# A ConvNeXt block with a gate: 8-channel convolution matrices read in one piece, four buffers, and another order of loads

## The chip, the cores and the metric

The kernel runs on one core of a Trainium2 chip. The metric is device time in microseconds (us). The program has five engines that matter: TensorE (PE, matmuls and the weight loads that go with them, PEld), VectorE (DVE), ScalarE (ACT), GpSimd (POOL) and SyncE (SP, which here only issues DMAs). Each works through its own instructions in order, and they meet by semaphores. DMAs run on 16 DMA engines that the core's queues share.

## The reference

Input x is 32 images of 384 channels and 28 x 28 pixels, float32. The first layer is a ConvNeXt block:

```python
y = conv_general_dilated(x, dw_w, padding=[(3, 3), (3, 3)], feature_group_count=C)  # 7x7, each channel alone
y = y.transpose(0, 2, 3, 1) + dw_b
y = layernorm(y) * ln_g + ln_b
y = gelu(y @ w1 + b1)                      # 384 -> 1536
gx = sqrt(sum(y * y over pixels)); nx = gx / (mean(gx) + eps)
y = grn_g * (y * nx) + grn_b + y
y = y @ w2 + b2                            # 1536 -> 384
x = x + y.transpose(0, 3, 1, 2)
```

The second layer takes mean, maximum and minimum of each channel's plane, forms logits from them with small matrices (W1, W2_1, W2_2, W3, Wfc) and returns sigmoid(logits + x).

## The kernel before

The kernel has two stages. The first computes the depthwise convolution of all images and writes it to a scratch tensor in HBM. The second goes through the images one by one: normalisation, the product with w1, GELU, the response norm, the product with w2, the gate. Both big products use a scheme with fewer multiplications, which needs sums of blocks of w1 and w2 (15 sums each, `UPSTEPS` and `STEPS`). These sums ("forms") are made in the first stage by POOL (`form_w`) and stored to the scratch tensors `u1d` and `u2d`. The change touches the first stage only.

**The convolution as matmuls.** For one channel a plane is cut into strips of 4 rows (`RW`), 7 strips an image; rows are padded to 32 columns, so a strip is 128 numbers, on the 128 partitions. For one channel the seven strips of all 32 images form the moving operand, 128 x 224. The output strip is a matrix times the strip itself (L309), plus a matrix times the next strip (L310, only 96 output rows wide), plus a matrix times the strip before (L313). All three are windows of one banded 128-row table whose row p is one and the same row of numbers, shifted by p. That row is written once for each channel to the scratch tensor `fs` (448 floats a channel, mostly zeros, built in `tab` from the 7x7 weights), and `load_t` (L199) reads it with a step of one element from partition to partition. One `load_t` brings the matrices of 8 channels (`TC`) into one of three `tmat` buffers: for each partition 8 pieces of 320 floats, behind 32 columns that are set to zero once.

**Steps and blocks.** The main loop has 48 steps of 8 channels; four steps are a block of 32 channels (`XC`). In each step PE does 24 convolution products, and ACT (L327) and DVE (L319) evict them from PSUM, with the bias `dwb` added, into `yc`, which is stored to `yd` every second step (the last two such stores go to `yl`).

**Turning x.** x comes from HBM as groups `xi` of 32 channels x 4 images (392 KB, `load_x`, four buffers); 8 groups are a block. POOL copies a group into a padded buffer `xpad` (`pad_x`, L237, two buffers), PE transposes it in two parts of 4 and 3 strips (`turn_x`, L248), and DVE copies each from PSUM into `xt` (L253). Before the main loop the first 8 groups are turned; in the loop two groups of the next block are turned in each step, between the convolution's products.

**Order.** The program is written as one sequence, and a scheduler puts each engine's instructions in an order by data and priority. DMAs of this stage are issued by SP, in order. SP starts with dww (the 7x7 weights), cv (five vectors of 384, in pieces of 4 bytes), dwb, the first xi, three stores to fs, one xi, two tmat loads, two xi, w1s (all of w1, 2304 KB), eight xi, w2s (all of w2) and fv (three vectors of 1536). In the loop the load of the matrices of step s + 2 is issued at step s. Step s makes one form, of w1 in even steps and of w2 in odd ones, from step 4 to 33. awt, w22b and wfc, small tensors for the gate, are loaded behind the stage in the program's text.

Of the kernel before, what the change touches and what calls it, by code (L numbers as in the profile page):

```python
# [8 lines left out]
F32 = mybir.dt.float32  # L9
AF = mybir.ActivationFunctionType  # L10
# [3 lines left out]
P = 128  # L14
C = 384
CB = C // P
FF = 4 * C
FB = FF // P
# [4 lines left out]
R = 8  # L23
# [8 lines left out]
PW = P // RW  # L32
XC = 32
TC = 8
YC = 16
NB = P // XC
REACH = 3 * PW
MW = P + 2 * REACH
FL = MW + P
NLAST = XC // YC  # L40
# [41 lines left out]
NS = len(STEPS)  # L82
# [19 lines left out]
KT = FB // 3  # L102
# [11 lines left out]
def convnext_gate_kernel(  # L114
# [13 lines left out]
    nc = tc.nc  # L128
    B = x.shape[0]
    N = NJ * B  # L130

    const = ctx.enter_context(tc.tile_pool(name="const", bufs=1))
# [7 lines left out]

    fs = [dram.tile([P, FL], F32, name=f"fs_{cb}") for cb in range(CB)]
    NY = C // YC
# [10 lines left out]
    cv = const.tile([P, 5, CB], F32, name="cv")  # L153
    nc.sync.dma_start(cv, cvec.rearrange("v (cb p) -> p v cb", p=P))
    _, lng_t, lnb_t, b2_t, w21_t = (cv[:, i, :] for i in range(5))
    fv = const.tile([P, 3, FB], F32, name="fv")
    b1_t, gg_t, gb_t = (fv[:, i, :] for i in range(3))
    ones_f = const.tile([P, P], F32, name="ones_f")
    nc.gpsimd.memset(ones_f, 1.0 / FF)
    eps_t = const.tile([P, 1], F32, name="eps_t")  # L160
    nc.gpsimd.memset(eps_t, EPS)
# [5 lines left out]
    with ExitStack() as one:  # L167
        tp = one.enter_context(tc.tile_pool(name="tp", bufs=1))
        xip = one.enter_context(tc.tile_pool(name="xip", bufs=4))
        xtp = one.enter_context(tc.tile_pool(name="xtp", bufs=2))  # L170
# [4 lines left out]

        w1s = tp.tile([P, CB, FF], F32, name="w1s")
        w2s = tp.tile([P, FB, C], F32, name="w2s")
        tab = tp.tile([P, CB, FL], F32, name="tab")
        nc.vector.memset(tab, 0.0)

        t0 = REACH + P - 1 - 3 * PW - 3
        for cb in range(CB):
            nc.vector.tensor_copy(
                tab[:, cb, t0 : t0 + 7 * PW].rearrange("p (y x) -> p y x", x=PW)[:, :, :7],
                dww[:, cb, :].rearrange("p (y x) -> p y x", x=7),
            )
            nc.sync.dma_start(fs[cb], tab[:, cb, :])

        NT2 = 3
        T0 = P - REACH
        tmat = [tp.tile([P, TC, T0 + MW], F32, name=f"tmat_{i}") for i in range(NT2)]
        for t in tmat:
            nc.gpsimd.memset(t[:, :, :T0], 0.0)
        dwb = tp.tile([P, C], F32, name="dwb")
        nc.sync.dma_start(dwb, cvec[0:1, :].broadcast_to([P, C]))
        NK = C // TC

        def load_t(s):  # L200
            base = fs[s * TC // P]
            c0 = s * TC % P
            nc.sync.dma_start(
                tmat[s % NT2][:, :, T0:],
                bass.AP(
                    tensor=base.tensor,
                    offset=base.offset + c0 * FL,
                    ap=[[1, P], [FL, TC], [1, MW]],
                ),
            )  # L210
# [29 lines left out]

        def turn_x(i, h, xt):

            g = i % NG
            xv = xt.rearrange("p c (j b) -> p j c b", j=NJ)
            j0, j1 = 4 * h, min(NJ, 4 * h + 4)
            pt = psx.tile([P, 4, P], F32, tag="pt", name=f"pt_{i}_{h}")
            for j in range(j0, j1):
                nc.tensor.transpose(  # L248
                    pt[:, j - j0, :],
                    xpad[i % NPAD][:, j * RW : (j + 1) * RW, :].rearrange("p r w -> p (r w)"),  # L250
                    ident,
                )
            nc.vector.tensor_copy(  # L253
                xv[:, j0:j1, :, g * NB : (g + 1) * NB],
                pt[:, : j1 - j0, :].rearrange("p j (c q) -> p j c q", q=NB),
            )

        def new_xt(k):
            return xtp.tile([P, XC, N], F32, tag="xt", name=f"xt_{k}")

        w1v = w1s.rearrange("p k (t m c) -> p t k m c", m=3, c=P)
        w2v = w2s.rearrange("p (t k) (m c) -> p t k m c", k=3, m=CB)

# [10 lines left out]

        for s in range(2):
            load_t(s)
        for i in range(4):
            load_x(i)
        nc.sync.dma_start(w1s, w1.rearrange("(cb p) f -> p cb f", p=P))
        xt = new_xt(0)  # L280
        for i in range(NG):
            pad_x(i)
            if i + 4 < GT:
                load_x(i + 4)
            for h in range(2):
                turn_x(i, h, xt)
        nc.sync.dma_start(w2s, w2.rearrange("(fb p) c -> p fb c", p=P))
        nc.sync.dma_start(fv, fvec.rearrange("v (fb p) -> p v fb", p=P))
        SK = XC // TC
        GS = NG // SK  # L290
        for s in range(NK):
            k, si = divmod(s, SK)
            if s + 2 < NK:
                load_t(s + 2)
            if si == 0:
# [8 lines left out]
            for c2 in range(TC // 2):  # L304
                pc = psc.tile([P, 2, 256], F32, tag="pc", name=f"pc_{s}_{c2}")
                for ci in range(2):
                    c = 2 * c2 + ci
                    xc = xt[:, si * TC + c, :]
                    nc.tensor.matmul(pc[:, ci, :N], t[:, c, P : 2 * P], xc, start=True, stop=False)  # L309
                    nc.tensor.matmul(  # L310
                        pc[:REACH, ci, : N - B], t[:, c, 2 * P :], xc[:, B:], start=False, stop=False
                    )
                    nc.tensor.matmul(  # L313
                        pc[:, ci, B:N], t[:, c, :P], xc[:, : N - B], start=False, stop=True
                    )
# [18 lines left out]
                if xn is not None:  # L334
                    g, h = divmod(si * (TC // 2) + c2, 2)
                    i = (k + 1) * NG + g
                    if h == 0:
                        pad_x(i)
                        if i + 4 < GT:
                            load_x(i + 4)  # L340
                    turn_x(i, h, xn)
# [19 lines left out]
            if si == SK - 1:  # L361
                xt = xn
            i = s // 2 - 2
            if 0 <= i < NS:
                if s % 2 == 0:
                    form_w(f"u1_{i}", w1v, UPSTEPS[i][1], u1d[:, :, i, :].rearrange("t p c -> p t c"))
                else:
                    form_w(
                        f"u2_{i}", w2v, STEPS[i][1], u2d[i].rearrange("p (t c) -> p t c", c=P)
                    )  # L370

# [19 lines left out]
    nc.vector.memset(gate, 0.0)  # L391
    awt = const.tile([P, 2, CB, R], F32, name="awt")
    nc.sync.dma_start(awt, aw.rearrange("v (cb p) r -> p v cb r", p=P))
    nc.vector.tensor_scalar(gate[:, 0, :, 0:R], awt[:, 0], 1.0 / NT, None, ALU.mult)
    nc.vector.tensor_copy(gate[:, 2, :, 2 * R : 3 * R], awt[:, 1])
    w22b = const.tile([P, R], F32, name="w22b")
    nc.sync.dma_start(w22b, w22.broadcast_to([P, R]))
    grp = const.tile([P, CB, R], F32, name="grp")
# [14 lines left out]
    nc.vector.tensor_copy(gate[:, 1, :, R : 2 * R], grp_b)  # L413
    wfc = const.tile([3 * R, C], F32, name="wfc")
    nc.sync.dma_start(wfc, wfcT)

# [424 lines left out]
```

## Time and profile before

| | us |
|---|---|
| median of 3 runs (3228.82 to 3229.85) | 3229.32 |
| profiled execution, its own time | 3229.09 |
| its span | 3227.3 |
| first convolution matmul (L309) starts | 36.02 |
| last one starts (the second stage's first transposes at 512.29) | 507.5 |
| DMA, share of 16 engines' time / GB/s, 0 to 36 us | 0.85 / 289 |
| the same, 36 to 75.67 us (first block) | 1.00 / 329 |
| the same, 530 us to the end | 0.43 / 137 |

The profile shows one execution, engine by engine; the time of a run is a little longer than the span, by 1.8 us here. A row of the timeline gives start, duration, engine, line, operation, output<-input and count, and in brackets how long the engine stood idle before it and what released it. A row of waits gives the waiting engine and line, what it waited for, us in total, how many times, and the longest. A DMA is shown on its issuing queue (SPq) while it is issued; its data land later: 7.8 us after the issue for tmat in the median, 8.4 for xi, 11.5 for yd.

### The profile page before, as it was taken

To read this page: it belongs to the slowest core of one execution; us is meant where nothing else is said; L and a number is where in the kernel's file an instruction comes from. 1 tells how busy PE (TensorE), PEld (TensorE's weight loads), DVE (VectorE), ACT (ScalarE), POOL (GpSimd) and SP (SyncE) were. 2 spreads that over 40 slices of the span, in tenths; PEclk is the share of its full clock that TensorE was granted. 3 is DMA by queue.
4 is the path that set the end of the run, shared out by engine and by line. 5 is a ranking of instruction groups with operands and counts; after the bars stand their busy time and mean duration, and the time that the engine had idled before them with its cause. 6 is when DMAs were issued, how large, how long until landed. Compare 5 with 4: busy or idle time off the path is not lost.

```text
span 3227.3 us, 35684 instructions
## 1 busy us (share of the span) xinstructions
PE 3177.9 (98%) x12352; PEld 2011.9 (62%) x12352; DVE 1674.7 (52%) x3447; ACT 1881.7 (58%) x3024; POOL 1604.6 (50%) x813
## 2 busy tenths in 40 slices
PE   7999998999999999999999999999999999999998
PEld 6999996555555555555555555555555555555555
DVE  3444335555555555555555555555555555555553
ACT  1222224866666666666666666666666666666662
POOL 2455311555555555555555555555555555555555
PEclk9999998999999999999999999999999999999999
DMA  9999986434444444444444444444444444444333
GB/s 310 342 333 332 317 283 207 129 112 143 141 142 139 136 132 139 142 132 142 145 134 143 145 134 144 134 143 145 145 131 137 131 135 142 141 142 140 123 103 125
DMA packets 300150, 534.10 MB, mean 165 GB/s; under 512 B 121004, under 2 KB 179908, under 8 KB 296900
## 3 DMA queue, kind: packets, MB, share of 16 engines
q1 hardware_dynamic: 287572, 494.51, 47.1%
q10 hardware_dynamic: 12400, 37.33, 3.4%
q8 instruction: 98, 1.61, 0.2%
q14 instruction: 80, 0.66, 0.1%
HBM read 440.65 MB, written 91.13 MB: 165 GB/s over the span
## 4 chain that ended last, share of the span: by engine, by line
PE 87%; ACT 1%; DVE 1%; issue 0%; ACTq 0%; DVEq 0%
PE ph_A L549 13%; PE ph_B L549 13%; PE pz_A L646 11%; PE pz_B L646 10%; PE pz_C L646 5%; PE pz_E L646 5%; PE ph_C L549 5%; PE pz_F L646 3%; PE pz_G L646 3%; PE pz_D L646 3%; PE ph_D L549 3%; PE ph_H L549 3%; PE ph_F L549 3%; PE py L475 2%; PE pc L309 2%; PE pc L310 1%
## 5 line engine op out<-in xcount | busy, mean ns | idle before, releaser
L621 POOL TENSOR_TENSOR d_v<-d_u,y 128x1568 f32<-128x1568 f32 x32 | 112.3, 3511 | 759.5 <-PE pz_B L646 735.4
L524 ACT ACTIVATE y<-y,fv 128x784 f32<-128x784 f32 x384 | 346.7, 941 | 214.5 <-DVE y L564 213.8
L457 ACT ACTIVATE y<-y,fv,gsc 128x784 f32<-128x784 f32 x378 | 358.6, 1027 | 29.9 <-DVE gsc L591 29.9
L327 ACT ACTIVATE yc<-pc,dwb 128x224 f32<-128x224 f32 x192 | 103.7, 642 | 401.1 <-PE pc L313 301.8
L530 ACT ACTIVATE junk<-y 128x784 f32<-128x784 f32 x384 | 326.6, 851 | 5.0
L621 POOL TENSOR_TENSOR d_p<-y 128x1568 f32<-128x1568 f32 x31 | 109.1, 3518 | 434.6 <-ACT y L457 434.6
L549 PE MATMUL ph_A<-af,u 128*128 128x392 f32 x768 | 314.0, 503 | 5.4 <-DVE af L515 5.3
L549 PE MATMUL ph_B<-af,u 128*128 128x392 f32 x768 | 311.3, 493 | 0.3 <-ACT y L556 0.3
L646 PE MATMUL pz_A<-y,u 128*128 128x392 f32 x768 | 268.8, 492 | 0.0
L621 POOL TENSOR_TENSOR y<-d_v,y 128x1568 f32<-128x1568 f32 x64 | 223.5, 3514 | 2.5
L549 PEld LDWEIGHTS ph_A<-af,u 128*128 128x128 f32 x768 | 136.4, 190 | 135.2 <-ACT y L556 57.4
L549 PE MATMUL ph_A<-acc,u 128*128 128x392 f32 x512 | 216.3, 504 | 0.0
L309 PE MATMUL pc<-xt,tmat 128*128 128x224 f32 x768 | 209.3, 354 | 4.9 <-issue 4.9
L549 PE MATMUL ph_B<-acc,u 128*128 128x392 f32 x512 | 213.6, 499 | 0.1
L549 PEld LDWEIGHTS ph_B<-af,u 128*128 128x128 f32 x768 | 145.3, 190 | 109.2 <-DVE y L560 9.6
L646 PEld LDWEIGHTS pz_A<-y,u 128*128 128x128 f32 x768 | 145.8, 190 | 106.4
L556 ACT ACTIVATE y<-ph_A 128x392 f32<-128x392 f32 x256 | 124.7, 487 | 145.2 <-PE ph_A L549 145.1
L560 DVE TENSOR_TENSOR y<-y,ph_A 128x392 f32<-128x392 f32 x128 | 71.9, 562 | 238.9 <-PE ph_A L549 224.6
L446 ACT ACTIVATE sd<-mv,eps_t 128x7 f32<-128x7 f32 x32 | 9.6, 300 | 314.3 <-DVE mv L441 314.3
L515 POOL TENSOR_TENSOR af<-af,acc 128x392 f32<-128x392 f32 x186 | 186.8, 1018 | 4.9
L313 PE MATMUL pc<-xt,tmat 128*128 128x192 f32 x768 | 187.6, 326 | 0.0
L310 PE MATMUL pc<-xt,tmat 128*96 128x192 f32 x768 | 187.6, 326 | 0.0
(153 smaller groups left out, 6903.5 us busy)
## 6 DMA issues: line engine op xcount, KB each, us to landing
u<-u1d SPq DMA_DIRECT2D x128, 960.0 KB, 4.6
u<-u2d SPq DMA_DIRECT2D x480, 256.0 KB, 2.7
tmat<-fs SPq DMA_DIRECT2D x48, 1280.0 KB, 7.8
yd<-yc SPq DMA_DIRECT2D x22, 1792.0 KB, 11.5
yi<-yd SPq DMA_DIRECT2D x32, 1232.0 KB, 6.9
xi<-in_x SPq DMA_DIRECT2D x96, 392.0 KB, 8.4
x<-in_x SPq DMA_DIRECT2D x32, 1176.0 KB, 5.6
out<-x ACTq DMA_DIRECT2D x31, 1176.0 KB, 5.0
```

Of the source, the lines that this page charges most:

```text
L309: nc.tensor.matmul(pc[:, ci, :N], t[:, c, P : 2 * P], xc, start=True, stop=False)
L310: nc.tensor.matmul(pc[:REACH, ci, : N - B], t[:, c, 2 * P :], xc[:, B:], start=False, stop=False)
L313: nc.tensor.matmul(pc[:, ci, B:N], t[:, c, :P], xc[:, : N - B], start=False, stop=True)
L327: nc.scalar.activation(yc[:, :, :, cy + ci].rearrange("p b j -> p j b"), pc[:, ci, :N].rearrange("p (j b) -> p j b", j=NJ), AF.Identity, b ...
L457: eng.activation(out, in_, AF.Identity, bias=add, scale=mul)
L515: eng.tensor_tensor(d, o[in0], o[in1], op)
L524: nc.scalar.activation(y, y, AF.Gelu, bias=b1_t[:, f : f + 1], scale=1.0)
L530: nc.scalar.activation(junk, ys[b][:, f, :], AF.Square, accum_out=ssqs[b][:, f : f + 1])
L549: nc.tensor.matmul(banks[bk][:, :NH], wt[:, i, :], o[opnd], start=(first == 1), stop=True, skip_group_check=True,)
L556: nc.scalar.activation(d, p, AF.Identity)
L621: nc.gpsimd.tensor_tensor(d, o[in0], o[in1], op)
L646: nc.tensor.matmul(pz[:, :NH], wt[:, t, :], o[opnd][:, t, :], start=(first == 1 and t == 0), stop=(t == KT - 1), skip_group_check=True,)
```

## The change

- **fs** is one scratch tensor of 385 rows of 355 floats. The 32 columns of zeros in front of a matrix are part of the row, and the row ends with the last weight (`SN` = 199, `S0` = 156). The 385th row is zeros, since the last partition reads past the 384th. The table is built with one copy for six rows of weights and one for the seventh, and its four stores are issued by ACT.
- **load_t** reads 8 rows as one run of 2840 floats (11360 bytes) for each partition: 128 pieces, not 1024. The zero columns come with it, so the memsets of tmat go. There are four tmat buffers, and the load of step s + 3 is issued at step s.
- **ws** takes the place of w1s and w2s: w1 is loaded into it at step 2, its 15 forms are made in steps 4 to 18, w2 is loaded into the same place at step 19, its forms are made in steps 22 to 36.
- **Order of the first loads**: dww, six xi, tmat 0, four xi, tmat 1, dwb, four xi, tmat 2, tmat 3. There are six xi buffers. fv, cv, both halves of awt, w22b and wfc are loaded in steps 4 to 9.
- **One-element copies by POOL** into the destination hold back such a load until the instruction that wrote the copied element is done: tmat 1 to 3 by a pad, the weights and vectors by the first eviction of the last `yc`.
- In the first 8 groups the second part's copy from PSUM is done by ACT (`turn_x` with `eng`).

```diff
+T0 = P - REACH
+SN = 6 * PW + 7
+S0 = T0 + REACH + P - 1 - 3 * PW - 3
-FL = MW + P
+FL = S0 + SN
...
-    fs = [dram.tile([P, FL], F32, name=f"fs_{cb}") for cb in range(CB)]
+    fs = dram.tile([C + 1, FL], F32, name="fs")
...
-    nc.sync.dma_start(cv, cvec.rearrange("v (cb p) -> p v cb", p=P))
...
-        xip = one.enter_context(tc.tile_pool(name="xip", bufs=4))
+        xip = one.enter_context(tc.tile_pool(name="xip", bufs=6))
...
-        w1s = tp.tile([P, CB, FF], F32, name="w1s")
-        w2s = tp.tile([P, FB, C], F32, name="w2s")
+        ws = tp.tile([P, CB * FF], F32, name="ws")
...
+        NT2 = 4
+        tmat = [tp.tile([P, TC, FL], F32, name=f"tmat_{i}") for i in range(NT2)]
         nc.vector.memset(tab, 0.0)
+        nc.scalar.dma_start(fs[C : C + 1, :], tab[:1, 0, :])
         for cb in range(CB):
             nc.vector.tensor_copy(
-                tab[:, cb, t0 : t0 + 7 * PW].rearrange("p (y x) -> p y x", x=PW)[:, :, :7],
-                dww[:, cb, :].rearrange("p (y x) -> p y x", x=7),
+                tab[:, cb, S0 : S0 + SN - 7].rearrange("p (y x) -> p y x", x=PW)[:, :, :7],
+                dww[:, cb, :42].rearrange("p (y x) -> p y x", x=7),
             )
-            nc.sync.dma_start(fs[cb], tab[:, cb, :])
-        NT2 = 3
-        tmat = [tp.tile([P, TC, T0 + MW], F32, name=f"tmat_{i}") for i in range(NT2)]
-        for t in tmat:
-            nc.gpsimd.memset(t[:, :, :T0], 0.0)
+            nc.vector.tensor_copy(tab[:, cb, S0 + SN - 7 :], dww[:, cb, 42:])
+            nc.scalar.dma_start(fs[cb * P : (cb + 1) * P, :], tab[:, cb, :])
...
-        def load_t(s):
-            base = fs[s * TC // P]
-            c0 = s * TC % P
-            nc.sync.dma_start(
-                tmat[s % NT2][:, :, T0:],
+        def load_t(s, eng=nc.sync):
+            eng.dma_start(
+                tmat[s % NT2].rearrange("p c m -> p (c m)"),
                 bass.AP(
-                    tensor=base.tensor,
-                    offset=base.offset + c0 * FL,
-                    ap=[[1, P], [FL, TC], [1, MW]],
+                    tensor=fs.tensor,
+                    offset=fs.offset + s * TC * FL,
+                    ap=[[1, P], [1, TC * FL]],
                 ),
             )
...
-        for s in range(2):
-            load_t(s)
-        for i in range(4):
+        AHEAD = 6
+        for i in range(AHEAD):
             load_x(i)
-        nc.sync.dma_start(w1s, w1.rearrange("(cb p) f -> p cb f", p=P))
         xt = new_xt(0)
         for i in range(NG):
             pad_x(i)
-            if i + 4 < GT:
-                load_x(i + 4)
+            if i == NG - AHEAD:
+                load_t(0)
+            if i == NG // 2:
+                nc.gpsimd.tensor_copy(tmat[1][:, 0, :1], xpad[i % NPAD][:, 0, :1])
+                load_t(1)
+                nc.sync.dma_start(dwb, cvec[0:1, :].broadcast_to([P, C]))
+            if i + AHEAD < GT:
+                load_x(i + AHEAD)
             for h in range(2):
-                turn_x(i, h, xt)
-        nc.sync.dma_start(w2s, w2.rearrange("(fb p) c -> p fb c", p=P))
-        nc.sync.dma_start(fv, fvec.rearrange("v (fb p) -> p v fb", p=P))
+                turn_x(i, h, xt, (nc.vector, nc.scalar)[h])
+        later = {
+            2: (
+                ws.rearrange("p (cb f) -> p cb f", f=FF),
+                w1.rearrange("(cb p) f -> p cb f", p=P),
+            ),
...
+            9: (wfc, wfcT),
+        }
...
-            if s + 2 < NK:
-                load_t(s + 2)
+            if s + 3 < NK:
+                if s == 0:
+                    for i in range(2, 4):
+                        nc.gpsimd.tensor_copy(tmat[i][:, 0, :1], xpad[i % NPAD][:, 0, :1])
+                        if i == 2:
+                            load_t(i)
+                load_t(s + 3)
+            if s in later:
+                dst, src = later[s]
+                first = dst[:, :1] if len(dst.shape) == 2 else dst[:, 0, :1]
+                nc.gpsimd.tensor_copy(first, yc[: dst.shape[0], 0, 0, :1])
+                nc.sync.dma_start(dst, src)
...
-                        pc[:REACH, ci, : N - B], t[:, c, 2 * P :], xc[:, B:], start=False, stop=False
+                        pc[:REACH, ci, : N - B], t[:, c, 2 * P : T0 + MW], xc[:, B:], start=False, stop=False
...
-            i = s // 2 - 2
+            i = s - U1
             if 0 <= i < NS:
-                if s % 2 == 0:
-                    form_w(f"u1_{i}", w1v, UPSTEPS[i][1], u1d[:, :, i, :].rearrange("t p c -> p t c"))
-                else:
-                    form_w(f"u2_{i}", w2v, STEPS[i][1], u2d[i].rearrange("p (t c) -> p t c", c=P))
+                form_w(f"u1_{i}", w1v, UPSTEPS[i][1], u1d[:, :, i, :].rearrange("t p c -> p t c"))
+            i = s - U2
+            if 0 <= i < NS:
+                form_w(f"u2_{i}", w2v, STEPS[i][1], u2d[i].rearrange("p (t c) -> p t c", c=P))
```

## The prediction

> **What bounds the kernel now.** I read the page first: its busy row, its rows by slice and its chain of waits.
>
> ```profile
> PE 3177.9 (98%) x12352; PEld 2011.9 (62%) x12352; DVE 1674.7 (52%) x3447; ACT 1881.7 (58%) x3024; POOL 1604.6 (50%) x813
> ...
> PE   7999998999999999999999999999999999999998
> ...
> DMA  9999986434444444444444444444444444444333
> ```
>
> TensorE (PE) is busy in 3177.9 of 3227.3 us, so at most 49.4 us can come out without less matrix work, and the change leaves the convolution's products as they are. A slice is 80.7 us: the idle time lies in slice 1 and around slices 7 and 8. The second row to see is DMA: full in the first six slices, 0.3 to 0.5 later. So the conv stage (up to 508 us, where the last L313 ends) has PE and DMA both near full; the rest has only PE. Next the waits of PE. From 36 to 530 us:
>
> ```profile
> PE ph_A L549 <- DVE af L515: 5.3, 1, 5.3
> PE pc L309 <- issue: 4.9, 11, 1.1
> PE py L475 <- ACT yn L457: 4.6, 2, 4.3
> PE pt L248 <- POOL xpad L237: 1.8, 1, 1.8
> ```
>
> The first and third lie after 508 us, in code that the change leaves alone. No wait on a tmat load appears: matrices are never late. Then the timeline of the first 37 us, PE, POOL and SP rows:
>
> ```profile
> 2.91 0.64 SPq L227 DMA_DIRECT2D xi<-in_x  x1
> 8.52 1.00 SPq L203 DMA_DIRECT2D tmat<-fs  x2
> 13.42 0.59 SPq L279 DMA_DIRECT2D w1s<-in_w  x1
> 8.81 1.76 PE L248 MATMUL pt<-ident,xpad 128*128 128x128 f32 x7 [8.81 <-POOL xpad L237]
> 20.88 0.84 POOL L237 COPY xpad<-xi 128x784 f32<-128x784 f32 x1 [9.45 <-DMA xi<-in_x]
> 27.45 1.49 POOL L270 TENSOR_SCALAR u<-w1s 128x512 f32<-128x512 f32 x1 [4.74 <-DMA w1s<-in_w]
> 29.79 6.32 PE L248 MATMUL pt<-ident,xpad 128*128 128x128 f32 x35 [4.77 <-POOL xpad L237]
> 36.02 0.65 PE L309 MATMUL pc<-xt,tmat 128*128 128x224 f32 x2
> ```
>
> The first convolution matmul starts at 36.02. It needs eight groups of x padded, turned and copied (the ninth is turned ahead of it in PE's order). The third group waited 9.45 us for its DMA behind two tmat loads; then POOL, which works in order, sat 4.74 us at a weight form that had been put ahead of the pads, until w1s had landed. Last, a table of stretches (us; then busy PE, PEld, DVE, ACT, POOL; granted clock, DMA share, GB/s):
>
> ```profile
> 11.00:18.00 7.00, 1.76 (x7) 1.36 (x7) 1.36 (x3) 0.00 (x0) 0.43 (x1) 1.00 1.03 354
> 19.00:29.00 10.00, 3.25 (x14) 2.85 (x14) 2.40 (x4) 0.00 (x0) 3.23 (x4) 1.00 1.02 413
> 75.67:115.34 39.67, 39.29 (x248) 37.94 (x248) 16.07 (x25) 8.66 (x16) 12.05 (x12) 1.00 0.99 351
> 523.00:528.50 5.50, 5.50 (x9) 2.94 (x10) 0.33 (x1) 1.49 (x3) 0.00 (x0) 0.51 1.03 388
> ```
>
> The first is mostly tmat traffic in pieces of 1280 bytes, the second x and w1s in rows of 3136 and 6144 bytes. A block of four steps (32 channels) takes 39.67 us, PE full.
>
> **The start.** Removed from in front of x on SP: cv, dwb, three fs stores, two tmat loads and w1s. Up to 36 us the queue listing counts 10.39 MB. In the new order what must land before the first matmul is nine x groups (9 x 0.401 = 3.61 MB), the fs rows (385 x 1420 bytes = 0.55 MB), tmat 0 (128 x 11360 bytes = 1.45 MB) and dww (0.08 MB): 5.69 MB. At 413 GB/s that is 13.8 us. Bytes begin about 1.7 us after the first issue at 0.79 (dww lands 2.0 us after its own), so at 2.5: 16.3. One hole: tmat 0 stands in SP's queue before x groups 7 to 10 and waits until the fs stores, now issued by ACT, have landed. These go out at about 3.5 to 5 us (after dww, as at L183) and took 4.8 us to land, so tmat 0 is issued near 9.5, when SP's six earlier x loads are nearly done; DMA may stand for 2 us. The ninth group lands at 18.3, the eighth at 17.3. The eighth then takes 0.84 us on POOL, 1.76 on PE (the 8.81 row) and about 0.7 for its copy: start at 20.7. Half of the copies of these groups go to ACT. No row shows that copy on ACT; the near one is its eviction acc<-py 128x448, 1.34 us for two, so 0.67 for 128x384, against 0.69 and 0.54 on DVE. Bounds 0.5 and 1.1 (the strided L327 takes 0.64 for 224): once at the end, so 0.7 is taken. ACT has no other work there but its table load (1.28 us).
>
> [...] The trace agrees in the 523 us row (0.51 granted for 5.5 us, after 5.29 us of idleness) and, in durations, at 8.81: 0.25 us for each transpose against 10 in 1.09 us later. While tmat 0 moves PE idles some 4 us, so the turns of groups 7 to 9 and the first matmuls run slow. Before, 6.3 us of transposes warmed PE up first. [...] by the 523 row 2.8; part of it is in the 1.76 already. I add 0.8: effective start 21.5, gain **36.0 - 21.5 = 14.5 us** (bounds 8 to 18). dwb follows tmat 1 and lands near 24; the first eviction is due at about 23. What queues behind it is ACT's evictions and DVE's turns, and four pc banks cover 8 us, so nothing is charged.
>
> **The convolution stage.** PE's rows are unchanged (L310 still 96 wide), 472 us from first to last. What must hold is DMA. A block loads 4 x 1.31 + 8 x 0.401 (x) + 2 x 1.835 (yd) + 4 x 0.262 (forms) = 13.17 MB now, which gives 332 GB/s, as the table's 329 to 351; afterwards 4 x 1.454 makes it 13.75 MB, 346 GB/s. Whether this fits hangs on the tmat rate. [...] 11% more bytes cost 11% more time, 4.11 us a load at 354 against 3.70. The trace has 354 against 413 for longer rows[...]. [...] I take it; it is also close to the 413 row. DMA's block is now busy about 0.98 x 39.67 = 38.9 us, of which tmat 4 x 3.70 = 14.8; with 4 x 3.56 it is 38.3: it fits, and costs nothing. At the other end, 354, it is 24.1 + 16.4 = 40.5, 0.9 over in each block with forms; forms run in 30 of 48 steps, 7.5 blocks, so 6 us are lost. The fourth buffer (a load issued three steps ahead, not two) covers single late loads, not a lack of rate.
>
> The weights move into the stage: ws twice (2.36 MB, 5.7 us each at 413), fv, cv and small ones, with their one-element POOL copies (0.1 us as the memsets). They come at 0.26 MB a step saved (no forms in steps 0 to 3 and 19 to 21), and three steps of prefetched matrices (29 us) cover them. Uncovered, 5 us once each.
>
> POOL: forms come one a step. Now two can run back to back: 10.5 us without a pad from 335.42 on, which is PE's 1.8 us wait above. In the new order at most one five-term form, 1.49 + 4 x 1.27 = 6.6 us, stands between pads (two pairs of short forms, 4.3 us, aside). A pad buffer is free half a step, 4.9 us, before it is due, and the form can start just after the previous pad, half a step earlier than that. So **1.8 us** go. The tmat memsets (0.81 us) lie in POOL's idle start: nothing.
>
> **Sum.** 14.5 + 1.8 = 16.3, less 0.8 for the loads that crowd steps 2 to 9: 15.5. The profiled run is 3229.09 us by its own clock, span 3227.3; span 3211.8, run 3213.6. The median shown is 0.2 above that run: **3213.8**.
>
> **Rivals.** (a) The forecast, 0.68. (b) The start moves less: fs stores on ACT's queue share with x, tmat 0 is issued late, PE cold; start at 28, gain 8 + 1.8 - 0.8 = 9: 3220. For it: the fs landing of 4.8 us. 0.12. (c) More: no hole, start 18.5, and half of the 4.9 us of "issue" gaps go: 17.5 + 1.8 + 2.4: 3207.6; 0.07. (d) Slower: DMA becomes the bound. All partitions of a load read nearly the same 11 KB of HBM, in long runs at once; if that gives 300 GB/s, a load takes 4.85 us, a block 24.1 + 19.4 = 43.5, 3.8 over, 7.5 times = 28.7; less 15.5: 3242.5. It decides below 330 GB/s for tmat (2.07 us over a block). For it: DMA is at 0.97 to 1.0 already. Against it: the old loads read the same bytes together at 354. 0.08. (e) The order changes but the start doesn't, DMA being full from 3 us on: 3227.5 with the POOL wait gone. Against it: 10.4 MB are moved before 36 us, 5.7 needed. 0.05.
>
> A measurement here can tell about 0.2%, 6.5 us, from no change. Faster: a, b, c: 0.87; same 0.05; slower 0.08. The range is 3204 to 3224: it takes in a, b and c and leaves out d and e.
>
> **What would show it.** First L309-type matmul (now L344) at 20 to 22 us; tmat issue to landing under 7.8 us in mid-stage, DMA share in blocks at most as now; last conv matmul near 492; the 1.8 us wait on xpad gone; nothing changed after it. Wrong if PE waits for tmat, or if POOL waits for x in mid-stage.

## The result, and the profile after

| us | before | after | difference |
|---|---|---|---|
| median of 4 runs each on one chip | 3229.59 (3228.82 to 3230.48) | 3217.57 (3216.49 to 3218.74) | -12.0 |
| profiled execution, its own time | 3229.09 | 3216.78 | -12.3 |
| its span | 3227.3 | 3215.1 | -12.2 |
| first convolution matmul starts | 36.02 | 24.40 | -11.6 |
| last convolution matmul row starts | 507.53 | 495.69 | -11.8 |
| from there to the end of the span | 2719.8 | 2719.4 | -0.4 |

The ratio of the times is 0.9963, with a 95% interval from 0.9945 to 0.998. The prediction was 3213.8 in a range of 3204 to 3224: the sign and the range held, and 12.0 us came of the 15.5 that its sum had.

The third column says where. All but 0.6 us of the gain are there when the first convolution matmul starts. Between the first and the last of them the stage takes 471.3 us, against 471.5 before. So two things have to be explained: why the start came at 24.40 and not at 20.7, and why the stage gave 0.2 us and not the 1.0 that the sum left in it (1.8 less 0.8). The 0.4 behind the stage is within what that part varies by in the runs below (2718.8 to 2720.7 us).

From the page of the kernel after, the rows that were read of before (busy time of PE and the other engines; PE and DMA in tenths by slice of 80.4 us):

```profile
PE 3174.8 (99%) x12352; PEld 2009.1 (62%) x12352; DVE 1669.3 (52%) x3442; ACT 1886.1 (59%) x3032; POOL 1607.1 (50%) x821
...
PE   8999998999999999999999999999999999999998
...
DMA  9999985444444444344444444444444444444333
```

PE is 3 us less busy and the span 12 us shorter: its idle time fell from 49 to 40 us. The first digit of its row is 8 and was 7: that is the slice in which the gain lies. The waits of PE, from 15 to 520 us (engine, line, what it waited for: us in total, times, longest):

```profile
PE pt L248 <- POOL xpad L237: 6.0, 1, 6.0
PE ph_A L576 <- DVE af L542: 5.4, 1, 5.4
PE pc L344 <- issue: 4.9, 11, 1.1
PE py L502 <- ACT yn L484: 4.6, 2, 4.3
PE pc L344 <- DVE yc L354: 1.5, 1, 1.5
```

Three of them were there before. The first lies in the start, where the kernel before had such waits too (8.5 and 4.8 us). The 1.8 us wait on xpad in mid-stage is gone, as predicted; in its place stands the last row, a wait on an eviction by DVE (L354 is the L319 of before). No wait on a tmat load appears. The start itself, in rows of the timeline of ACT's queue, DVE, SP's queue, POOL and PE (in brackets the idle time before and what ended it):

```profile
3.41 1.89 ACTq L199 DMA_DIRECT2D fs<-tab  x3
4.68 0.19 DVE L194 COPY tab<-dww 128x42 f32<-128x42 f32 x1 [1.14 <-DMA fs<-tab]
11.94 0.34 SPq L203 DMA_DIRECT2D tmat<-fs  x1
12.37 2.57 SPq L227 DMA_DIRECT2D xi<-in_x  x4
19.87 0.84 POOL L237 COPY xpad<-xi 128x784 f32<-128x784 f32 x1 [6.19 <-DMA xi<-in_x]
20.89 0.84 POOL L237 COPY xpad<-xi 128x784 f32<-128x784 f32 x1
20.76 3.28 PE L248 MATMUL pt<-ident,xpad 128*128 128x128 f32 x16 [6.04 <-POOL xpad L237]
24.40 0.65 PE L344 MATMUL pc<-xt,tmat 128*128 128x224 f32 x2 [0.36 <-ACT xt L258]
```

SP issued its first six x loads by 6.6 us and then did nothing for 5.3 us: the load of tmat 0 is next in its order, and it waits for the fs stores. x groups 7 to 10 stand behind it, though they need nothing from it. Why the stores are late can be seen in the second row: before the last part of the table is filled, DVE waits 1.14 us for the store of the zero row, because that store reads a row of the same table. The part that waits is the one that holds this row, channels 0 to 127, and tmat 0 reads rows of this part only: its store goes out last of the three, at about 5.0 us, and tmat 0 leaves 0.09 us after that store has landed. The three take 6.4 to 6.9 us to land. Six groups were turned before this gap, so the pads at 19.87 and 20.89 are the seventh and the eighth; the eighth group's load landed at 20.70. The table of stretches for this time (from:to; length, then busy PE, PEld, DVE, ACT, POOL; granted clock, DMA share, GB/s):

```profile
2.50:8.00 5.50, 2.04 (x10) 2.04 (x11) 1.38 (x7) 1.73 (x3) 1.68 (x2) 1.00 0.91 261
8.00:11.00 3.00, 2.20 (x13) 1.56 (x11) 1.16 (x2) 0.88 (x3) 1.46 (x2) 1.00 1.05 408
11.00:13.00 2.00, 1.28 (x10) 1.04 (x11) 0.92 (x2) 0.84 (x2) 1.35 (x4) 1.00 0.60 194
13.00:18.00 5.00, 1.67 (x14) 1.20 (x12) 1.38 (x2) 0.98 (x2) 0.68 (x1) 0.87 0.90 295
20.00:24.00 4.00, 3.24 (x16) 3.04 (x16) 1.28 (x2) 0.63 (x2) 2.76 (x6) 0.56 1.07 445
```

Up to 18 us only the stretch from 8 to 11 comes near the 413 GB/s of the sum. The last row has the clock: 0.56 granted while the last groups are turned, as the mean of 0.50 up to 23.5 us and 1.00 from there on.

### The profile page after: what moved, and what is told of

Read it like the earlier page. It is cut to its first block, busy times and chain, and to the rows that moved or that the text cites. A ratio compares the mean times of both kernels' runs of the same rounds, so it can differ in the third digit from the quotient of the medians.

```text
span 3215.1 us, 35678 instructions
## 1 busy us (share of the span) xinstructions
PE 3174.8 (99%) x12352; PEld 2009.1 (62%) x12352; DVE 1669.3 (52%) x3442; ACT 1886.1 (59%) x3032; POOL 1607.1 (50%) x821
## 4 chain that ended last, share of the span: by engine, by line
PE 98%; DVE 1%; ACT 1%; DMA 1%; issue 0%; SPq 0%; ACTq 0%; POOL 0%; DVEq 0%; POOLq 0%
PE ph_A L576 14%; PE ph_B L576 13%; PE pz_A L673 11%; PE pz_B L673 10%; PE pz_C L673 5%; PE pz_E L673 5%; PE ph_C L576 5%; PE pc L344 5%; PE pc L345 4%; PE pc L348 4%; PE pz_F L673 3%; PE ph_D L576 3%; PE ph_H L576 3%; PE ph_F L576 3%; PE pz_G L673 3%; PE pz_D L673 3%
## 5 line engine op out<-in xcount | busy, mean ns | idle before, releaser
L237 POOL COPY xpad<-xi 128x784 f32<-128x784 f32 x96 | 80.6, 841 | 254.4 <-PE pt L248 188.1
```

## The experiments

My theory, once the result was known, was that the order of the loads makes the whole gain, and that what is missing from it is SP's wait at tmat 0: the later that load is issued, or the more x groups stand behind it, the later the start. Piece length and the fourth buffer would then be worth nothing, since the stage has PE full and no wait on a matrix. The rivals: the start is set by bytes and rate, so that another order of the same loads moves it little; long rows free DMA in the stage and carry part of the gain; ACT's copies are what brought the start forward.

All edits are against the kernel after, but for one that starts from the kernel before. In the three sets of runs the kernel before took 3230.40, 3229.39 and 3229.68 us. "Rest" is the span less the start (the first convolution matmul): it tells a start that moved from a stage that changed.

| | median us (lowest to highest) | ratio to before, 95% | start | span | rest |
|---|---|---|---|---|---|
| before | 3229.59 | | 36.02 | 3227.3 | 3191.3 |
| after | 3217.57 (3216.49 to 3218.74) | 0.9963 [0.9945, 0.998] | 24.40 | 3215.1 | 3190.7 |
| e1_x_first | 3212.87 (3212.28 to 3213.35) | 0.9946 [0.9929, 0.9962] | 21.66 | 3211.0 | 3189.3 |
| e8_fs_on_sp | 3213.89 (3212.84 to 3214.39) | 0.9951 [0.9937, 0.9966] | 21.38 | 3212.7 | 3191.3 |
| e10_zero_row | 3215.65 (3214.29 to 3217.19) | 0.9957 [0.9943, 0.9972] | 22.58 | 3213.1 | 3190.5 |
| e4_turns_on_dve | 3218.03 (3217.36 to 3218.98) | 0.9965 [0.9952, 0.9978] | 25.9 | 3216.7 | 3190.8 |
| e3_order_alone | 3217.71 (3217.43 to 3218.09) | 0.9961 [0.9946, 0.9976] | 23.42 | 3215.4 | 3192.0 |
| e2_short_rows | 3219.26 (3216.84 to 3220.21) | 0.9964 [0.9951, 0.9977] | 24.43 | 3215.1 | 3190.7 |
| e6_w2_pieces | 3217.27 (3216.74 to 3218.09) | 0.9960 [0.9945, 0.9975] | 24.60 | 3215.6 | 3191.0 |
| e5_three_buffers | 3222.86 (3222.01 to 3224.22) | 0.9979 [0.9971, 0.9988] | 24.69 | 3221.8 | 3197.1 |
| e11_tmat_after_four | 3211.92 (3211.47 to 3212.21) | 0.9945 [0.9928, 0.9961] | 20.45 | 3210.5 | 3190.1 |
| e12_tmat_after_three | 3212.20 (3211.89 to 3213.08) | 0.9946 [0.9932, 0.9961] | 20.18 | 3210.5 | 3190.3 |
| e14_with_w2_pieces | 3211.13 (3209.79 to 3212.34) | 0.9943 [0.9928, 0.9957] | 19.42 | 3208.8 | 3189.4 |

Read down the last column: it stays within 1.5 us of the kernel after, but for one experiment. Apart from that one, what moves the span is the start. A part of what is left is work that changes sides: the more transposes PE has done before the first product (63 before, 58 after, 70 in e1 and e11), the fewer fall into the stage, at 0.11 us each (in e5 and e8 a run of four takes 0.60 us there, one of three 0.49).

### The start

**e1_x_first** puts tmat 0 one group later in the program and makes it wait for a pad; in SP's order all four x loads that stood behind it are then ahead of it.

```diff
-            if i == NG - AHEAD:
+            if i == 3:
+                nc.gpsimd.tensor_copy(tmat[0][:, 0, :1], xpad[i % NPAD][:, 0, :1])
                 load_t(0)
```

> The changed kernel, with tmat 0 held back until the fourth group of x is padded, so that SP issues x groups 7 to 10 ahead of it. Theory A (a wait in SP's queue: x 7 was issued at 12.37 us only because tmat 0 stood before it and waited for the fs stores until 11.94): groups 7 to 10 land by 15, tmat 0 by about 18, the first convolution matmul moves from 24.4 to 18 to 20 us, the run from 3217.6 to 3211 to 3214. Rival C (bytes: whatever the order, the same 5.7 MB must land first): start stays at 23 to 25 us, run within 1.5 us of 3217.6.

The start moved to 21.66, by 2.7 us, and the span by 4.1. Most of the other 1.4 us is in the stage: 12 more transposes are done before the first product, and PE is busy 464.1 us in the stage, not 465.4. SP's queue and PE's first convolution row show what was not foreseen:

```profile
6.91 0.53 SPq L292 DMA_DIRECT2D dwb<-in_cvec  x1
10.10 3.21 SPq L227 DMA_DIRECT2D xi<-in_x  x4
13.37 1.17 SPq L203 DMA_DIRECT2D tmat<-fs  x2
...
21.66 0.65 PE L345 MATMUL pc<-xt,tmat 128*128 128x224 f32 x2 [1.30 <-DMA tmat<-fs]
```

x 7 now stands ahead of tmat 0 and still goes out at 10.10 only, not at about 7: SP had issued dwb by 7.44, and the buffer that x 7 takes was free from 5.92 us on, after the first pad. What held it for 2.7 us no row shows. The fs stores took 6.7 us to land in this run; issued from 3.4 us on, as in the kernel after, the first of them landed at about 10.1, so a tie to that store is likely, though not shown. So x is first in the order and still comes late. The theory is right in kind and less in size; the last wait of the start is now on tmat 0, not on x.

**e8_fs_on_sp** issues the fs stores from SP, among the x loads, and gives the zero row a tile of its own, so that the table no longer waits for its store. **e10_zero_row** does the second of these alone and leaves the stores on ACT.

```diff
-        nc.scalar.dma_start(fs[C : C + 1, :], tab[:1, 0, :])
+        zrow = tp.tile([1, FL], F32, name="zrow")
+        nc.vector.memset(zrow, 0.0)
...
-            nc.scalar.dma_start(fs[cb * P : (cb + 1) * P, :], tab[:, cb, :])
+            nc.sync.dma_start(fs[cb * P : (cb + 1) * P, :], tab[:, cb, :])
+        nc.sync.dma_start(fs[C : C + 1, :], zrow)
```

> The changed kernel, with the fs stores issued by SP among the first x loads (zero row first, from a small tile of its own; the three others after the second x load), not by ACT. SP then has x 7 and 8 ahead of tmat 0. Theory A (the late fs landing, 6.6 us on ACT's queue beside x, is what holds tmat 0 until 11.9 and with it x 7 to 10): the stores land in about 3.5 us as in the kernel before with the new order, by 7.5; tmat 0 is issued by 9.5, first convolution matmul at 18.5 to 20.5, run 3210.5 to 3213.5. Rival (nearly all of the wait is the moving of bytes, not the queue): start at 22 to 24.4, run 3215 to 3217.6.

> The changed kernel, with the zero row of fs stored from a tile of its own, so that no table copy waits for that store; all fs stores still on ACT. If the 1.1 us that DVE waits before the last table copy is what delays the stores, tmat 0 is issued about 1.2 us earlier (10.7) and the start moves to 23.2, the run to 3216.4. If the landing beside x is what takes the time, tmat 0 stays at 11.5 to 12 and the run at 3217 to 3218.

ACT's and SP's queues of e10:

```profile
3.20 1.45 ACTq L200 DMA_DIRECT2D fs<-tab  x3
9.19 0.34 SPq L205 DMA_DIRECT2D tmat<-fs  x1
```

With e10 tmat 0 is issued at 9.19, which is 2.75 us earlier and about where the prediction had it (9.5), and the start comes 1.8 us earlier. The wait for the zero row thus costs more than its 1.14 us on DVE: without it the store that tmat 0 needs is the first of the three and lands at 9.11, while the last lands only at 12.06. The stores still took 5.9 to 8.0 us to land. With e8 they took 6.7 us in the median in spite of the other queue, so my number of 3.5 was wrong: the queue is not what makes them slow. tmat 0 went out at 11.00, not 9.5, and yet the start came at 21.38, since in that order x 7 and 8 are ahead of it. PE's rows of e8:

```profile
12.78 8.02 PE L250 MATMUL pt<-ident,xpad 128*128 128x128 f32 x42 [1.82 <-POOL xpad L239]
21.38 0.65 PE L346 MATMUL pc<-xt,tmat 128*128 128x224 f32 x2 [0.58 <-ACT xt L260]
```

PE turns groups without a gap up to the start, where the kernel after has 6.04 us of idle time. So what counts for the start is x behind tmat 0, more than the moment of tmat 0.

**e4_turns_on_dve** gives ACT's copies of the first groups back to DVE.

```diff
-                turn_x(i, h, xt, (nc.vector, nc.scalar)[h])
+                turn_x(i, h, xt)
```

> The changed kernel, with all copies of the first eight groups on DVE, none on ACT. Each group's two copies then take 1.2 us in a row. Theory A: the last groups arrive a DMA apart, so only the last pair counts: the start moves from 24.4 to 24.6 to 25.6, the run to 3217.6 to 3218.8. Rival (the ACT copies carry part of the gain): start at 26 or later, run 3219.5 or more.

The start is at 25.9, 1.5 us later; tmat 0 went out 0.9 later in that run, at 12.82, so ACT's share of the start is between 0.6 and 1.5. Some 0.6 of it comes back in the stage, since 63 transposes are done before the first product and not 58. DVE's rows of e4:

```profile
22.78 1.20 DVE L256 COPY xt<-pt 128x512 f32<-128x512 f32 x2 [6.82 <-PE pt L248]
24.27 1.20 DVE L256 COPY xt<-pt 128x512 f32<-128x512 f32 x2 [0.29 <-PE pt L248]
25.77 1.16 DVE L256 COPY xt<-pt 128x512 f32<-128x512 f32 x2 [0.30 <-PE pt L248]
```

The last groups come all at once when x lands, and on one engine their copies stand one after another. In the time of the run this is within the spread of the two kernels: 3218.03 against 3217.57.

### Order, pieces and buffers, one by one

**e3_order_alone** starts from the kernel before and takes the order only: x first, tmat 0 after the first four x loads, w1, w2, fv and cv in steps 2 to 5, dwb behind tmat 1. The tables, the pieces of 1280 bytes, three tmat buffers, four xi buffers, the two places for w1 and w2 and DVE's copies stay.

```diff
-    nc.sync.dma_start(cv, cvec.rearrange("v (cb p) -> p v cb", p=P))
...
-        for s in range(2):
-            load_t(s)
...
-        nc.sync.dma_start(w1s, w1.rearrange("(cb p) f -> p cb f", p=P))
...
+            if i == 2:
+                load_t(0)
+            if i == NG // 2:
+                nc.gpsimd.tensor_copy(tmat[1][:, 0, T0 : T0 + 1], xpad[i % NPAD][:, 0, :1])
+                load_t(1)
+                nc.sync.dma_start(dwb, cvec[0:1, :].broadcast_to([P, C]))
```

> The kernel before, with the new order of loads alone: x first, tmat 0 after four x groups, dwb after tmat 1, w1s and w2s in steps 2 and 3, fv and cv in steps 4 and 5. Old rows, three tmat buffers, four x buffers, two weight places, all copies on DVE. Theory A: order carries nearly all of the gain, first convolution matmul at 23 to 27 us, run 3217 to 3221. Rival B: the long rows and fourth buffer are needed for it, PE waits in steps 2 to 8 while 4.7 MB of weights land: 3224 to 3230.

It takes 3217.71, as the whole change does (3217.57); against the kernel before of its own set the ratio is 0.9961, and 0.9963 for the whole change. Its start is 23.42, by another way: the fs stores land in 3.5 us beside four x loads in all, not six, and tmat 0 is issued at 6.70. Order is therefore enough for the whole gain, with short pieces and three buffers. This does not make the other parts worthless in every order; it says that this gain needs none of them.

**e2_short_rows** keeps everything of the kernel after and reads the matrices in 8 pieces of 1416 bytes.

```diff
-                tmat[s % NT2].rearrange("p c m -> p (c m)"),
+                tmat[s % NT2][:, :, : FL - 1],
...
-                    ap=[[1, P], [1, TC * FL]],
+                    ap=[[1, P], [FL, TC], [1, FL - 1]],
```

> The changed kernel, with each tmat load in 8 pieces of 1416 bytes for each partition, and nothing else changed. Theory A (the gain is the start; tmat is never late in mid-stage, so piece size is hidden): run within 2 us of 3217.6, DMA's share of the blocks with forms up to 1.0, no wait of PE for tmat; start within 1.5 us of 24.4. Rival B (DMA binds: 13.7 MB a block at the old 354 GB/s for tmat): 0.9 us more in each of 7.5 blocks, 3223 to 3226, with waits on tmat or on xpad.

Span and start are those of the kernel after within 0.1 us, and so are the waits, but for 0.3 us more on a pad in the start. The median of its runs is 1.7 us higher, but the runs overlap, and against the kernel before of its own set the ratio is the same (0.9964 and 0.9963). What the pieces cost can be read from DMA alone, in the stretch from 120 to 420 us, where 30 matrix loads run (queue: packets, MB, share of 16 engines). Before, after, and e2:

```profile
q1 hardware_dynamic: 51107, 97.46, 94.8%
```

```profile
q1 hardware_dynamic: 24981, 105.83, 93.7%
```

```profile
q1 hardware_dynamic: 52556, 105.91, 96.0%
```

After and e2 move the same bytes, and the long pieces save 2.3 points of 300 us: 6.9 us over 30 loads, 0.23 us each. That is less than the 0.55 of the prediction (4.11 less 3.56), and in the profiled run all of it is hidden. Against before, DMA moves 8.6% more bytes in 1.1 points less of its time: 376 GB/s per full share against 343. Pieces of 1416 bytes already reach 368, so the length of the pieces carries only a quarter of that rise. What carries the rest I have not separated; the loads in this stretch are not the same either, since w2's 2.36 MB fall into it in the kernel after and in e2, and not in the kernel before.

### The stage

**e6_w2_pieces** loads w2 in three pieces, at steps 19, 20 and 21, in place of one load of 2.36 MB at step 19. It asks where the wait on DVE at 253 us comes from. DVE's rows of the kernel after show the wait itself:

```profile
249.34 1.78 DVE L256 COPY xt<-pt 128x512 f32<-128x512 f32 x3 [5.99 <-PE pt L248]
252.11 0.56 DVE L256 COPY xt<-pt 128x384 f32<-128x384 f32 x1 [0.99 <-PE pt L248]
252.59 1.67 DVE L354 TENSOR_TENSOR yc<-pc,dwb 128x448 f32<-128x448 f32 x2
```

In DVE's order two evictions (L354) stand behind a run of copies of turned groups. DVE waits 5.99 us for PE's transposes while products lie ready to be evicted; PE then finds no free bank and waits 1.5 us. That order is written before the program runs, by the scheduler, which had put the turns there late.

```diff
-            U2 - 3: (
-                ws.rearrange("p (fb c) -> p fb c", c=C),
-                w2.rearrange("(fb p) c -> p fb c", p=P),
-            ),
...
+            if U2 - 3 <= s < U2:
+                n = s - (U2 - 3)
+                w2p = ws[:, 4 * n * C : 4 * (n + 1) * C].rearrange("p (fb c) -> p fb c", c=C)
+                later[s] = w2p, w2.rearrange("(fb p) c -> p fb c", p=P)[:, 4 * n : 4 * n + 4]
```

> The changed kernel, with w2 loaded in three pieces of 0.79 MB, one in each of steps 19, 20 and 21. Theory A (PE's 1.5 us wait for DVE at 252 us comes from the evictions put behind turns in DVE's order around the one load of 2.36 MB): the wait shrinks below 0.8 us, the run gains 0 to 1.5: 3216 to 3217.6. Rival: the wait has nothing to do with w2 and stays at 1.5 us.

The wait on DVE is gone. "Issue" grew from 4.9 to 5.6 us, and the stage from first to last product took 470.3 us against 471.3. The time of the run is within the spread of the kernel after (3217.27 against 3217.57), so by itself this is not settled. With the better start it shows again: e12, below, needs 470.8 us from first to last product and has this wait; e14, which has the pieces of w2 in addition, needs 469.8 and doesn't. In both pairs PE does the same number of transposes in the stage. In the runs with this wait (after, e1, e2, e4, e8, e10, e11, e12) PE stands idle for 6.3 to 6.4 us between the first and the last product, in the two without it for 5.6 and 5.7. So the stage gain is shown, and at 1.0 us it is too small to be told in the time of a run. How a load of one piece leads the scheduler to that order isn't shown.

**e5_three_buffers** takes the fourth tmat buffer away; loads are issued two steps ahead.

```diff
-        NT2 = 4
+        NT2 = 3
...
-            if s + 3 < NK:
+            if s + 2 < NK:
...
-                load_t(s + 3)
+                load_t(s + 2)
```

> The changed kernel, with three tmat buffers and loads two steps ahead. Theory A (tmat is landed within 17 to 18.5 us at worst, against 19.8 us of two steps): start within 0.5 us of 24.4, no wait of PE on tmat longer than 1 us, run within 1.5 us of 3217.6. Rival (the fourth buffer is needed around the two weight loads): PE waits for tmat at about 60 and 240 us, together 2 to 6 us, run 3219.5 to 3224.

Neither theory has this. It is 5.3 us slower than the kernel after, and this is the one run whose rest changed: the stage takes 478.4 us, 7 more. Yet PE waits for no matrix here either; the longest landing of one was 14.5 us, and two steps are 19.8. Its waits of PE from 15 to 520 us:

```profile
PE pt L248 <- POOL xpad L237: 8.5, 2, 5.5
...
PE pt L248 <- DVE xt L256: 5.2, 12, 0.4
```

and DVE's rows from one of the places where PE waits:

```profile
184.04 0.95 DVE L351 TENSOR_TENSOR yc<-pc,dwb 128x448 f32<-128x448 f32 x1 [1.37 <-PE pc L345]
184.84 2.66 DVE L256 COPY xt<-pt 128x384 f32<-128x384 f32 x5
190.79 0.94 DVE L351 TENSOR_TENSOR yc<-pc,dwb 128x448 f32<-128x448 f32 x1 [3.29 <-ACT yc L359]
```

With three buffers the scheduler lays the turns in clumps: in ten places DVE's order has four or more turn copies with two evictions behind them, against one in the kernel after and none before. PE stands between its transposes for a copy of DVE. The longest single wait in the stage is another: 3.0 us for a pad, between 380 and 420 us. Some products are slower too: the longest at L341 and L342 take 0.577 and 0.524 us, where the kernel after has 0.457 and 0.326 at most for the same two. In all PE stands 4.1 us longer in the stage than in the kernel after and is busy 3.0 us longer, with the same number of transposes and products. A fourth buffer pays here, then, but through the order of the turns and not by covering late matrices. e3 has three buffers too and loses nothing of the kind, so it hangs on the combination; what in it makes the clumps I did not find.

### A better version

**e11_tmat_after_four** joins the zero row of e10 with the place of tmat 0 of e1, and also holds dwb back until a pad. **e12_tmat_after_three**, whose edit is shown, is the same with tmat 0 one group earlier. **e14_with_w2_pieces** is e12 with the pieces of w2 of e6.

```diff
-        nc.scalar.dma_start(fs[C : C + 1, :], tab[:1, 0, :])
+        zrow = tp.tile([1, FL], F32, name="zrow")
+        nc.vector.memset(zrow, 0.0)
...
+        nc.scalar.dma_start(fs[C : C + 1, :], zrow)
...
-            if i == NG - AHEAD:
+            if i == 2:
+                nc.gpsimd.tensor_copy(tmat[0][:, 0, :1], xpad[i % NPAD][:, 0, :1])
                 load_t(0)
...
+                nc.gpsimd.tensor_copy(dwb[:, :1], xpad[i % NPAD][:, 0, :1])
```

> The changed kernel, with both holes closed: the zero row of fs from a tile of its own, tmat 0 held back until the fourth group is padded (SP issues x 7 to 10 first), dwb held back until tmat 1. Theory A (the start is 2 to 3 us of late fs stores and 3 us of x behind tmat 0, and they overlap): x 10 issued by 11.5, tmat 0 by 12, landed by 19.5; start 19.5 to 21, run 3211 to 3213. Rival (bytes bind at 21.5, as both single edits show): 21.4 to 22, 3212.5 to 3214.

> The same with tmat 0 held until the third group is padded, so that it stands ahead of x 10, which the first matmul does not need. Theory A: tmat 0 issued near 10.7, landed by 17.5 to 18.5; then the ninth group, its pad and turns set the start, 19 to 20.5, run 3210.5 to 3212.5. Rival (bytes): as the one before within 0.5 us.

> The one before, with w2 in three pieces besides. If the order of evictions on DVE in steps 20 to 23 costs PE its 1.5 us, this is 1 to 1.5 us below it, 3209.5 to 3211.5; if such waits only move, it is the same within 0.7 us.

SP's queue and PE's last turns and first product of e11:

```profile
1.28 11.09 SPq L229 DMA_DIRECT2D xi<-in_x  x10
12.46 1.09 SPq L205 DMA_DIRECT2D tmat<-fs  x2
...
14.15 4.95 PE L250 MATMUL pt<-ident,xpad 128*128 128x128 f32 x35 [0.16 <-POOL xpad L239]
20.45 0.65 PE L348 MATMUL pc<-xt,tmat 128*128 128x224 f32 x2 [1.34 <-DMA tmat<-fs]
```

All ten x loads go out ahead of tmat 0 (though SP takes 11.09 us over the ten, where the kernel after takes 5.32 for six and 2.57 for four), DMA moves 422 GB/s from 12 to 20 us where the kernel after moves 294, PE turns 35 tiles in one piece, and the last wait is 1.34 us for tmat 0. One group earlier (e12) brings nothing that a run can tell. e14 has the shortest time of all: 3211.13, whose highest run (3212.34) is below the lowest of the kernel after (3216.49), and 18.5 us below before. Against e11 and e12 its runs overlap, and 0.8 of the 1.7 us that its span is below e12's lie in the start, where the two programs do not differ.

## Why the prediction came out as it did

**The step that was off is the size of the start.** Its mechanism held: the weights and vectors left the front, x goes first, and the first product starts when the eighth group has been turned and copied. The term that was mis-sized is the bytes' way to the eighth group: landing at 17.3 predicted, 20.70 measured. That is 3.4 of the 3.7 us by which the start came late; what follows took 3.7 us where the sum had 3.4.

- *The hole before tmat 0.* The sum had the fs stores out at 3.5 to 5 us and landed in 4.8, tmat 0 issued near 9.5, and 2 us in which DMA stands. The stores landed in 6.4 to 6.9 us, and the zero row held the one that tmat 0 needs; tmat 0 went out at 11.94.
- *The rate.* By 20.7 us, 5.65 MB had moved; the sum has 5.29 up to the eighth group (5.69 less 0.40), and the rest are parts of loads behind it, 0.9 us that the sum did not have. At 413 GB/s from 2.5 us on, 5.65 MB end at 16.2, so 4.5 us went elsewhere, where 2 were charged. The stretches above divide them, each by length x (1 - rate / 413): 2.0 from 2.5 to 8 us, at 261 GB/s with the fs rows beside x; 1.1 from 11 to 13, the hole, at 194; 1.4 from 13 to 18, with tmat 0 at 295 GB/s. So the charge for the hole itself was even too high; the full rate was assumed for two stretches that don't have it. e11 shows the last two as avoidable: it has the same 2.0 to 2.2 at first, none of the rest, and starts at 20.45.
- *The turns and the clock.* From the eighth group's landing to the first product the sum had 3.4 us (0.84, 1.76 and 0.7, with 0.1 from rounding), and 0.8 more for a slow clock behind the start, an estimate of mine (the row at 523 us, 5.5 us at 0.51, would give 2.8 in all). Measured from 20.70 to 24.40: 3.7. The granted clock was 0.50 from 17 us, in the 6.04 us for which PE stood idle, up to 23.5, and 16 transposes took 3.28 us, 0.205 each, against 0.144 in the 28 that e1 runs in 4.04 us at a clock of 1.00; ACT's copy took 0.49 us, not 0.7. The clock was back 0.9 us ahead of the first product, and the products after 24.40 have the durations that they had before (0.65, 0.49, 0.49). So the slow turns lie ahead of the start, where the 1.76 held most of their cost already, and the 0.8 behind it was a charge too many.

The sum of these: the start was 3.7 us later than 20.7 and the 0.8 behind it didn't come, 2.9 us of the 3.3 that the span is over its forecast (3215.1 against 3211.8); the stage adds 0.8, and the end gives 0.4 back. Rival (b) had this very mechanism, stores that share with x, tmat 0 late and PE cold, at about twice its size: it put the start at 28. The measured start lies halfway between the two, and so does the profiled run, 3216.78.

**POOL's 1.8 us** went, as predicted, since no two forms stand between pads any more. The step didn't say what is late next, and 1.5 us came back as a wait on DVE's order, around the one large load of w2. The 0.8 charged to the crowding of steps 2 to 9 wasn't seen: no wait lies there. Five transposes more than before also fall into the stage (614 against 609). Together this comes to -0.2 in the stage, not -1.0.

**DMA in the stage** fits, as predicted, and PE waits for no matrix. The 3.56 us a load of the sum, 408 GB/s for 1.454 MB, was an estimate of mine that no row showed; the nearest was the 413 GB/s of x and w1s. For long rows it had the sign and more than twice the size (0.55 us a load, measured 0.23): an eightfold length of the pieces is worth 2.3 points of DMA time here (96.0% against 93.7%). The sign that I named for it failed: tmat's landing was to be under 7.8 us and is 9.3; why is open, and an earlier issue alone doesn't explain it, since in e5, where the loads are issued one step later, it is 11.0. DMA's share did fall, from 94.8% to 93.7%.

**The fourth buffer** I had as cover for single late loads. No load was late with three either (e5); its worth, 5.3 us, is in the order of the turns.

**After the stage** nothing changed that the runs can tell, as predicted. The slower rival (d) asked for under 330 GB/s on tmat in mid-stage; it had a point for one load, tmat 0, at 295, and none for the stage.

## What to carry to other kernels

In a DMA queue that is worked in order, look at what stands behind each load that must wait: in the kernel after tmat 0 waited 5.2 us for a store, with four x loads behind it, and taking four x loads out from behind one matrix load was worth 2.7 us of the start (e1), and 4.0 with the zero row out of the way as well (e11). A rate from later in the kernel wasn't the rate of the first microseconds here: 261 GB/s from 2.5 to 8 us, where the fs stores go out beside x, against the 413 of 19 to 29 us before. So these are summed by themselves. Where a scheduler writes the order, a buffer more or less changes that order, and its worth is found only by looking at the order of each engine, not at the waits on the buffer.

## What the hardware showed that I had not expected

- A store of 0.18 MB to HBM took 5.9 to 8.0 us to land beside six to eight x loads, from ACT's queue as from SP's (after, e8, e10). In e3, with two x loads ahead of the stores and two behind them, it took 3.5; e8 too has two ahead, but four behind. That the number of loads in flight makes this is likely from these runs and not shown: e3 differs in the table's layout too.
- tmat 0, with the four x loads queued behind it, ran at 295 GB/s at a DMA share of 0.90, and in short pieces (e2) at 283; x and tmat in the order of e11 run at 433 in the same 13 to 18 us. In mid-stage a tmat load isn't slow (8.6 us to landing in the median from 120 to 420 us, 9.1 for an x load of a quarter of its size). Why the first is, stays open.
- x 7 in e1 went out 2.7 us after SP had issued the load ahead of it (10.10 against 7.44), with its buffer free since 5.92. That the landing of an fs store, at about 10.1 by the estimate above, released it is likely and not shown.
